# Crossbar transposes of 2048 columns made as two of 1024, and one batch's quantised activations transposed as pairs of bytes

## The chip, the cores and the metric

The kernel runs on one core of a Trainium2 chip. The metric is the device time of one execution in microseconds (us), the median over the runs. A core has five engines, each with an instruction stream of its own: TensorE (PE in the profile, with PEld for its weight loads), VectorE (DVE), ScalarE (ACT), GpSimd (POOL) and SyncE (SP). In this kernel SP issues every DMA, the transposes among them.

## The reference

There are two batches of 1024 tokens by 2048 features. A layer norm is followed by a product with a context matrix, both sides quantised to 0..255; then comes a second layer norm, and a linear layer with a routed LoRA (8 experts, rank 16, the best two). Both steps are added to x:

```python
def fake_quant(x, scale, zp):
    q = jnp.clip(jnp.round(x / scale + zp), 0.0, 255.0)
    return (q - zp) * scale

x = x + fake_quant(layernorm(x)) @ fake_quant(ctx)          # ctx: 2 x 2048 x 2048
y = layernorm(x)
w = top-2 weights of softmax(y @ W_router.T)                # 8 experts
h = einsum('td,erd->ter', y, lora_A)
x = x + y @ W_base.T + b_base + 2 * einsum('ter,eor,te->to', h, lora_B, w)
```

## The kernel before

Tokens go in 8 tiles of 128 (the `i` of the code), pairs of them in 4 (`p`); features and columns go in 16 chunks of 128 (`k`), outputs in blocks of 512 (`c`) or halves of 1024 (`cp`). Everything is done for batch 0 and then for batch 1, and the two overlap at the seam.

**First product.** `ln1` (L628 on) computes the statistics of one x tile (L408 on DVE, a Newton step at L644 that POOL does for all but the first four tiles of batch 0), quantises each half to bytes `q8` with `affine` (L387 if ACT does it, L392 to L398 on DVE), makes fp16 `qn` from them, and turns the tile over, so that features lie on partitions: `at_i`. For the first four tiles of batch 0 TensorE does that (`turn`, L690); for all others one `transpose` of 2048 columns (L377) goes through the crossbar of the DMA engines. In the profile the tiles are named without their numbers: `q`, `qn`, `at`. The context is loaded in pieces of 512 KB (`bs`), quantised to `u` and brought to fp16 as `b` (`load_b`). Batch 0 multiplies plainly (L723, 512 matmuls). Batch 1 uses one level of Strassen-Winograd: `half_sums` makes `as12` and `as4` from pairs of `at` (L797, profile name `as`), `half_diffs` makes `bt` from `b` (L814), and `gemm1w` multiplies (L843, banks `gX` and `gY`, 448 matmuls). The result is added to x as it leaves the bank (L752); squares for the next layer norm are summed on ACT (L771).

**Second product.** `y_prep` (from L888) normalises a pair of tiles and makes seven combinations `a11`, `a12`, `a22`, `s1` to `s4`. Each is split in `emit` into a high and a low fp16 part that stand side by side in a tile `nat` of 2048 columns, and one `transpose` makes a tile `y` from both. In the profile `nat_a` and `y_a` hold the `a` tiles and `nat_s` and `y_s` the `s` tiles. `hmm` multiplies the `a11`, `a12`, `s1`, `a22` tiles by the router and LoRA-A weights (L953 and L957, bank `ph`); `router` picks the experts and builds the weighted hidden tile `hh`, which another transpose turns into `hT`. `g2` is the linear layer, again by Strassen, with three fp16 products for each one (L1281, banks X and Y, 2688 matmuls), the LoRA part at L1297 and the sum into x at L1309. Its weights are prepared by `w_step` for each chunk and group: a load (`wc`, `wt`, `wb`, `wn`), on DVE some differences, a high part (L387 or L394) and a low part (L1091). L532 and L536 belong to a maximum over the LoRA weights that is taken once (`sm_bmax`, `bmax_row`).

**Order.** Nothing in the code says in which order the engines work. Each operation is added to a `Plan` as a task with an engine (or two, DVE and ACT, with a cost for each), the buffers that it reads and writes, sometimes in parts, and for matmuls a due time. `Plan.rank` gives every other task a due time backwards from its readers. `Plan.order` then runs a small model of the core: each engine takes the most urgent task that is ready and whose buffers fit into the slots (48 of 4 KB under tag `u`), and the task stays busy for its cost. The tasks are emitted in the order of their modelled starts, and that is the order of each engine's instructions. For DMAs the model keeps one shared stretch of transfers (`dma_free`, 0.82 us for each 1024 transposed columns) and up to 8 lanes. A transposing SP task is modelled as holding SP for 1.35 us and 0.22 more for each 1024 columns, and until 0.2 us before the latest landing of any DMA issued so far:

```python
if t.turn:
    end = max(end, land - 0.2)
dma_free = max(end + 0.2, dma_free) + t.dma
```

So a change of a cost or of a buffer's parts can move any instruction of SP, ACT and DVE.

Of the kernel before, what the change touches and what calls it, by code (L numbers as in the profile page):

```python
# [15 lines left out]
U8 = mybir.dt.uint8  # L16
AF = mybir.ActivationFunctionType
# [4 lines left out]
P = 128  # L22
# [21 lines left out]
MM = 0.216  # L44
LANES = 8
# [40 lines left out]
TURN_COST = 0.82  # L86
# [22 lines left out]
class Plan:  # L109
# [56 lines left out]
    def order(self):  # L166
# [7 lines left out]
        land = 0.0  # L174
# [44 lines left out]
        while todo:  # L219
# [8 lines left out]
            for eng in busy:  # L228
                while busy[eng] <= now:
                    pick = None  # L230
                    q = ready[eng]
                    for n, item in enumerate(q):
# [9 lines left out]
                        if t.dma is not None:  # L242
# [3 lines left out]
                            if len([x for x in lanes if x > now]) >= LANES:  # L246
                                break
# [19 lines left out]
                    if t.dma is not None:  # L267
                        if t.turn:
                            end = max(end, land - 0.2)
# [4 lines left out]
                        land = max(land, t.done)  # L274
                        lanes = [x for x in lanes if x > now] + [t.done]
# [27 lines left out]
def xattn_ffn_kernel(ctx, tc, x, cx, scal, wT, bias, arT, bT, out):  # L303
# [72 lines left out]
    def transpose(dst, src, r, w, cols, **kw):  # L376
        add("SP", 1.35 + 0.22 * cols / 1024, lambda: nc.sync.dma_start_transpose(dst(), src()),  # L377
            r=r, w=w, dma=TURN_COST * cols / 1024, turn=True, **kw)

    def affine(dst, src, n, r, w, scale=None, bias=None, only=None, **kw):  # L380
# [19 lines left out]
        durs = {"ACT": n * 0.00083 + 0.19 + 0.09 * ptrs, "DVE": n * 0.00053 + 0.145 + 0.06 * ptrs}  # L400
        if only:
# [226 lines left out]
    def ln1(S, b, i):  # L628
# [30 lines left out]
        qn = buf("u", [P, D], F16, f"qn_{n}", 2)  # L659
        for h in range(2):  # L660
            q8 = buf("q8", [P, HD], U8, f"q8_{n}_{h}")
            affine(q8.ap, xt[h].ap, HD, [xt[h], s], [q8],
                   scale=lambda: s.ap()[:, 10:11], bias=lambda: s.ap()[:, 12:13],
                   only=None if b == 0 and i < QBOTH else "ACT")
            affine(lambda h=h: qn.ap()[:, h * HD : (h + 1) * HD], q8.ap, HD, [q8], [(qn, [h])],
                   bias=nz1)
            if pe_turn:
                turn(aT, qn, h, n)
        if not pe_turn:
            transpose(aT.ap, qn.ap, [qn], [aT], D)  # L670
# [29 lines left out]
    def load_b(S, b, c):  # L700
        for j in range(4):
            bp = buf("u", [P, 4, C], F16, f"b_{b}_{c}_{j}", 2)
            S["b", c, j] = bp
            for h in range(2):
# [5 lines left out]
                         "(k p) n -> p k n", p=P), HD * 4, [s])  # L710
# [177 lines left out]
    def y_prep(S, b, p):  # L888
# [10 lines left out]
        def emit(o, t):  # L899
            n = buf("u", [P, 2, HD], F16, f"nat_{o}_{b}_{p}")  # L900
            y = buf("u", [P, 2, HK, P], F16, f"y_{o}_{b}_{p}")
            S["y", p, o] = y
            affine(lambda: n.ap()[:, 0], t.ap, HD, [t], [n])
            add("DVE", 1.22,
                lambda: nc.vector.tensor_tensor(
                    n.ap()[:, 1], t.ap(), n.ap()[:, 0], ALU.subtract), r=[t], w=[n])
            transpose(
# [559 lines left out]
```

## Time and profile before

| what | value |
|---|---|
| median of 3 runs | 921.09 us (920.28, 921.09, 923.07) |
| the profiled execution, its own time | 919.79 us |
| its span in the trace | 918.0 us |
| mean granted TensorE clock | 0.994 of full speed |
| DMA, mean over the span | 265 GB/s |
| `y_s<-nat_s` transposes | 32, median 4.7 us from issue to landing |
| `y_a<-nat_a` transposes | 24, median 5.1 us |
| `at<-qn` transposes | 12, median 5.8 us |
| `hT<-hh` transposes | 2, median 6.0 us |
| context loads `bs` | 64 of 512 KB, median 10.6 us |

The page of the profile shows one execution. Its first part gives the busy time of each engine as a share of the span. The timeline view lists the instructions of an engine in order: start, time, engine, line, operation, output and inputs with their shapes, how many of the same kind are put together on the row, and in brackets the idle time before it with what ended it. "SPq" rows are DMA issues on SP's queue; their time is how long SP itself was held, not how long the transfer took. The waits view adds up the idle time of an engine by what it waited for. Matmuls are pipelined, so that a row's duration can be longer than the distance to the next one.

### The profile page before, as it was taken

The page shows a single profiled execution, that of the slowest core. Times are in us where ns is not written, and L with a number is a line of the kernel's source. Part 1 is how long each engine was busy: PE and PEld are TensorE (multiplying, and loading weights), DVE is VectorE, ACT ScalarE, POOL GpSimd, SP SyncE. Part 2 cuts the span into 40 slices and gives each one's busy share as a digit, 9 for nine tenths or more (in the row PEclk, how much of TensorE's full clock was granted, in tenths as well). Part 3 has the DMA queues.
Part 4 walks back from the last instruction along what each step waited for, and adds up shares of the span by engine and source line. Part 5 has one row for each costly group of instructions (what it writes and reads, how often), then busy time and mean ns, then how long its engine had stood idle before and what let it go on. Part 6 is the DMA issues. An engine that isn't in the chain of part 4 may idle for free. (4 is left out here: it accounts for less than half of the span.)

```text
span 918.0 us, 12390 instructions
## 1 busy us (share of the span) xinstructions
PE 897.9 (98%) x4514; PEld 430.2 (47%) x4514; DVE 712.2 (78%) x1267; ACT 401.5 (44%) x458; POOL 66.1 (7%) x256
## 2 busy tenths in 40 slices
PE   7999999999999999999998999999999999999998
PEld 5444445474444444444443444647444444444443
DVE  7999998989598975999978998999835353799131
ACT  5999676516064321423892575863200121234000
POOL 0024220000000000002621003000000000000000
PEclk8999999999999999999999999999999999999999
DMA  9999999998999999999999946999995169793021
GB/s 321 387 385 284 314 289 251 180 225 267 235 332 321 391 393 374 380 381 342 315 319 243 366 179 158 243 230 211 307 260 186 58 203 389 245 353 127 12 91 47
DMA packets 230733, 243.11 MB, mean 265 GB/s; under 512 B 152848, under 2 KB 165136, under 8 KB 230672
## 3 DMA queue, kind: packets, MB, share of 16 engines
q1 hardware_dynamic: 230672, 242.33, 87.0%
q8 instruction: 35, 0.57, 0.2%
q14 instruction: 26, 0.21, 0.1%
HBM read 163.65 MB, written 41.94 MB: 224 GB/s over the span
## 5 line engine op out<-in xcount | busy, mean ns | idle before, releaser
L1281 PEld LDWEIGHTS <-y_s 128*128 128x128 f16 x1536 | 150.1, 98 | 183.4 <-issue 2.8
L1281 PE MATMUL X<-w,y_s 128*128 128x512 f16 x768 | 207.2, 379 | 2.0 <-DVE w L1091 2.0
L1281 PE MATMUL Y<-w,y_s 128*128 128x512 f16 x768 | 207.0, 379 | 0.0
L1281 PE MATMUL X<-w,y_a 128*128 128x512 f16 x768 | 189.2, 379 | 0.0
L1281 PEld LDWEIGHTS <-y_a 128*128 128x128 f16 x1152 | 112.0, 98 | 133.0 <-DMA y_a<-nat_a 1.3
L723 PE MATMUL g<-b,at 128*128 128x512 f16 x512 | 114.6, 384 | 4.1 <-ACT b L387 2.0
L387 ACT ACTIVATE w<-wb,gW 128x1024 f16<-128x1024 f32 (+1 forms) x48 | 51.5, 1076 | 121.5 <-DVE wb L1152 56.6
L1281 PE MATMUL Y<-w,y_a 128*128 128x512 f16 x384 | 103.2, 379 | 0.3 <-DMA y_a<-nat_a 0.3
L723 PEld LDWEIGHTS <-at 128*128 128x128 f16 x512 | 50.1, 99 | 64.4 <-issue 4.4
L1309 DVE SCALAR_TENSOR_TENSOR xr<-X,uW,xr 128x512 f32<-128x512 f32 x64 | 46.5, 746 | 30.4 <-PE X L1297 24.0
L1309 DVE SCALAR_TENSOR_TENSOR xr<-Y,uW,xr 128x512 f32<-128x512 f32 x42 | 31.1, 745 | 46.7 <-PE Y L1297 30.9
L1091 DVE SCALAR_TENSOR_TENSOR w<-wb,gW,w 128x1024 f16<-128x1024 f32 (+1 forms) x48 | 56.9, 1193 | 8.1 <-ACT w L387 7.8
L435 POOL TENSOR_TENSOR sm<-sm 128x1 f32<-128x1 f32 (+1 forms) x48 | 14.2, 296 | 487.2 <-DVE sm L421 484.7
L771 ACT ACTIVATE sq<-x,sm 128x1024 uint8<-128x1024 f32 x32 | 36.4, 1139 | 25.7 <-DVE x L752 16.7
L387 ACT ACTIVATE b<-u,nz 128x1024 f16<-128x1024 uint8 x41 | 45.7, 1138 | 1.8 <-DVE bt L814 0.8
L387 ACT ACTIVATE u<-bs,sc,rec 128x1024 uint8<-128x1024 f32 x31 | 38.0, 1233 | 15.4 <-DMA bs<-in_cx_dram 14.5
L408 DVE BATCH_NORM_STATS2 sm<-x 128x6 f32<-128x512 f32 x64 | 40.9, 683 | 4.8 <-DMA x<-in_x_dram 4.8
L387 ACT ACTIVATE w<-wt,gW 128x1024 f16<-128x1024 f32 x14 | 16.1, 1148 | 64.7 <-DVE wt L1138 41.6
L387 ACT ACTIVATE q<-x,sm 128x1024 uint8<-128x1024 f32 x30 | 35.7, 1229 | 13.3 <-POOL sm L644 8.6
L387 ACT ACTIVATE nat_s<-yt_a 128x1024 f16<-128x1024 f32 x30 | 31.1, 1050 | 19.4 <-DVE yt_a L912 13.2
L843 PEld LDWEIGHTS <-at 128*128 128x128 f16 x256 | 24.9, 98 | 31.0 <-issue 1.2
L912 DVE TENSOR_TENSOR yt_a<-yt_a,yt_a 128x1024 f32<-128x1024 f32 x32 | 38.6, 1220 | 0.0
(188 smaller groups left out, 1158.7 us busy)
## 6 DMA issues: line engine op xcount, KB each, us to landing
bs<-in_cx_dram SPq DMA_DIRECT2D x64, 512.0 KB, 10.6
wt<-in_wT_dram SPq DMA_DIRECT2D x64, 512.0 KB, 7.6
wn<-in_wT_dram SPq DMA_DIRECT2D x32, 512.0 KB, 9.0
x<-in_x_dram SPq DMA_DIRECT2D x30, 512.0 KB, 7.7
spill<-x SPq DMA_DIRECT2D x28, 512.0 KB, 4.4
xr<-spill SPq DMA_DIRECT2D x28, 512.0 KB, 8.1
wb<-in_wT_dram SPq DMA_DIRECT2D x24, 512.0 KB, 8.0
out_dram<-xr SPq DMA_DIRECT2D x24, 512.0 KB, 6.1
```

The costliest lines, as they stand in the source:

```text
L387: nc.scalar.activation(o, i, AF.Copy if c is None else AF.Identity, scale=1.0 if a is None else a, bias=0.0 if c is None else c,)
L408: nc.vector.bn_stats(st[:, 2 * h + c], b.ap()[:, c * C : (c + 1) * C])
L435: e.tensor_tensor(t, r, r, ALU.mult)
L723: nc.tensor.matmul(ps.ap(), aT.ap()[:, k, :], S["b", c, k // 4].ap()[:, k % 4, :], start=k == 0, stop=k == KT - 1,)
L771: nc.scalar.activation(sq.ap(), xb.ap(), AF.Square, bias=a[:, 22 + j : 23 + j], accum_out=a[:, 24 + 2 * j + h : 25 + 2 * j + h],)
L843: nc.tensor.matmul(ps.ap(), a()[:, 4 * h + k, :], w.ap()[:, k, :], start=fresh and h + k == 0, stop=h == 1 and k == 3, skip_group_check=True,)
L912: add("DVE", 1.22, lambda: nc.vector.tensor_tensor(dst.ap(), a.ap(), c.ap(), op), r=[a, c], w=[dst])
L1091: lambda: nc.vector.scalar_tensor_tensor(w.ap()[:, 1, lo:up], src(), g, w.ap()[:, 0, lo:up], ALU.mult, ALU.subtract),
L1281: nc.tensor.matmul(ps.ap(), y.ap()[:, a, k, :], w.ap()[:, q, j * C : (j + 1) * C], start=k == 0 and fresh and i == 0, stop=k == HK - 1 and ...
L1309: nc.vector.scalar_tensor_tensor(xs, ps.ap(), uW[:, cp : cp + 1], xs, ALU.mult, ALU.add)
```

## The change

A transpose never has more than 1024 columns. The late x tiles of batch 0, all `y` tiles and `hT` are turned over in two halves, each with its own part of the buffers, so that a reader of one half waits for that half alone. In `emit` the high half is issued before the low part is computed; the two halves of `y` are its high and its low part. In `router` the two halves are tiles 0 to 3 and 4 to 7, and the LoRA matmuls at L1297 name the half that they read.

For batch 1, x isn't brought to fp16 ahead of the transpose. ACT quantises both halves into one byte tile `q`; its 2048 bytes in a row are read as 1024 16-bit values and turned over once, so that a partition then holds two neighbouring features, byte by byte. Two `affine`s unpack every second byte into the fp16 tile `at`. The features therefore stand in another order within each group of 256, and batch 1's context rows are loaded in that order too, two neighbouring rows to a partition.

The planner's model gets new constants. A transpose holds SP for 1.5 us, and 1024 columns take 1.0 us of transfer in place of 0.82. SP is no longer held until the latest landing, only until there is room in a ring of 5, of which a transpose takes 2 and any other DMA 1. An unpack is costed at 0.75 us on DVE.

```diff
--- before.py
+++ after.py
@@ -14,6 +14,7 @@
 I32 = mybir.dt.int32
 U32 = mybir.dt.uint32
 U8 = mybir.dt.uint8
+U16 = mybir.dt.uint16
 AF = mybir.ActivationFunctionType
 ALU = mybir.AluOpType
 AX = mybir.AxisListType
@@ -42,6 +43,7 @@
          "sm": 4, "sm2": NP, "wacc": 1, "ps": 8}
 HORIZON = 120.0
 MM = 0.216
+SPREAD = .75
 LANES = 8
 DEPTH = 2.5
 NEAR = 45.0
@@ -83,7 +85,10 @@
 LAND = 2.1
 STORE_LAND = 1.15
 TURN_LAND = 0.65
-TURN_COST = 0.82
+TURN_COST = 1.0
+TURN_ISSUE = 1.5
+RING = 5
+TURN_RING = 2
 NEXT = {"DVE": 0.08, "ACT": 0.1}
 
 
@@ -171,7 +176,6 @@
         events = [0.0, 0.9]
         lanes = []
         dma_free = 1.2
-        land = 0.0
         lag = 0.0
         for t in self.tasks:
             t.left = len(t.preds)
@@ -243,7 +247,7 @@
                             if dma_free > now + DEPTH:
                                 wake(dma_free - DEPTH)
                                 break
-                            if len([x for x in lanes if x > now]) >= LANES:
+                            if len([x for x in lanes if x[0] > now]) >= LANES:
                                 break
                         if (eng == "DVE" and len(t.durs) > 1 and busy["ACT"] <= now
                                 and t.prio > -100):
@@ -266,13 +270,18 @@
                     end = now + t.dur
                     if t.dma is not None:
                         if t.turn:
-                            end = max(end, land - 0.2)
+                            room = RING - TURN_RING
+                            for at, n in sorted(lanes, reverse=True):
+                                room -= n
+                                if room < 0:
+                                    end = max(end, at)
+                                    break
                         dma_free = max(end + 0.2, dma_free) + t.dma
                         t.done = dma_free + (
                             TURN_LAND if t.turn else STORE_LAND if t.store else LAND
                         )
-                        land = max(land, t.done)
-                        lanes = [x for x in lanes if x > now] + [t.done]
+                        lanes = [x for x in lanes if x[0] > now]
+                        lanes.append((t.done, TURN_RING if t.turn else 1))
                     else:
                         t.done = end + 0.1
                         end -= NEXT.get(eng, 0.0)
@@ -374,10 +383,10 @@
             r=r, w=w, dma=nbytes * P / RATE, **kw)
 
     def transpose(dst, src, r, w, cols, **kw):
-        add("SP", 1.35 + 0.22 * cols / 1024, lambda: nc.sync.dma_start_transpose(dst(), src()),
+        add("SP", TURN_ISSUE, lambda: nc.sync.dma_start_transpose(dst(), src()),
             r=r, w=w, dma=TURN_COST * cols / 1024, turn=True, **kw)
 
-    def affine(dst, src, n, r, w, scale=None, bias=None, only=None, **kw):
+    def affine(dst, src, n, r, w, scale=None, bias=None, only=None, dve=None, **kw):
         ptrs = sum(v is not None and not isinstance(v, float) for v in (scale, bias))
 
         def fn(eng):
@@ -398,6 +407,8 @@
                 nc.vector.tensor_scalar(o, i, a, c, ALU.mult, ALU.add)
 
         durs = {"ACT": n * 0.00083 + 0.19 + 0.09 * ptrs, "DVE": n * 0.00053 + 0.145 + 0.06 * ptrs}
+        if dve:
+            durs["DVE"] = dve
         if only:
             return add(only, durs[only], lambda: fn(only), r=r, w=w, **kw)
         return add(durs, 0, fn, r=r, w=w, **kw)
@@ -656,18 +667,39 @@
             add("DVE", 0.6, lambda: rstd_seed(s, 1), w=[s])
             add("DVE" if fast else "POOL", 1.6 if fast else 4.0, newton, w=[s])
         aT = buf("u", [P, KT, P], F16, f"at_{n}", 2)
-        qn = buf("u", [P, D], F16, f"qn_{n}", 2)
-        for h in range(2):
-            q8 = buf("q8", [P, HD], U8, f"q8_{n}_{h}")
-            affine(q8.ap, xt[h].ap, HD, [xt[h], s], [q8],
-                   scale=lambda: s.ap()[:, 10:11], bias=lambda: s.ap()[:, 12:13],
-                   only=None if b == 0 and i < QBOTH else "ACT")
-            affine(lambda h=h: qn.ap()[:, h * HD : (h + 1) * HD], q8.ap, HD, [q8], [(qn, [h])],
-                   bias=nz1)
-            if pe_turn:
-                turn(aT, qn, h, n)
-        if not pe_turn:
-            transpose(aT.ap, qn.ap, [qn], [aT], D)
+        if b:
+            q = buf("u", [P, 2, D], U8, f"q_{n}", 4)
+            for h in range(2):
+                affine(lambda h=h: q.ap()[:, 0, h * HD : (h + 1) * HD], xt[h].ap, HD, [xt[h], s],
+                       [(q, [h])], scale=lambda: s.ap()[:, 10:11], bias=lambda: s.ap()[:, 12:13],
+                       only="ACT")
+            transpose(
+                lambda: q.ap()[:, 1].bitcast(U16).rearrange("p (k t) -> p k t", t=P),
+                lambda: q.ap()[:, 0].bitcast(U16), [(q, [0, 1])], [(q, [2, 3])], HD)
+            for h in range(2):
+                affine(
+                    lambda h=h: aT.ap()[:, h * HK : (h + 1) * HK, :].rearrange(
+                        "p (k s) t -> p k s t", s=2),
+                    lambda h=h: q.ap()[:, 1, h * HD : (h + 1) * HD].rearrange(
+                        "p (k t s) -> p k s t", t=P, s=2),
+                    HD, [(q, [2 + h])], [(aT, [h])], bias=nz1, dve=SPREAD)
+        else:
+            qn = buf("u", [P, D], F16, f"qn_{n}", 2)
+            for h in range(2):
+                q8 = buf("q8", [P, HD], U8, f"q8_{n}_{h}")
+                affine(q8.ap, xt[h].ap, HD, [xt[h], s], [q8],
+                       scale=lambda: s.ap()[:, 10:11], bias=lambda: s.ap()[:, 12:13],
+                       only=None if b == 0 and i < QBOTH else "ACT")
+                affine(lambda h=h: qn.ap()[:, h * HD : (h + 1) * HD], q8.ap, HD, [q8], [(qn, [h])],
+                       bias=nz1)
+                if pe_turn:
+                    turn(aT, qn, h, n)
+            if not pe_turn:
+                for h in range(2):
+                    transpose(
+                        lambda h=h: aT.ap()[:, h * HK : (h + 1) * HK, :],
+                        lambda h=h: qn.ap()[:, h * HD : (h + 1) * HD], [(qn, [h])], [(aT, [h])],
+                        HD)
         S["at", i] = aT
         if first:
             warm = bank("warm")
@@ -707,7 +739,7 @@
                 s = buf("u", [P, 2, C], F32, f"bs_{b}_{c}_{j}_{h}")
                 load(s, s.ap,
                      cx[b, k0 * P : (k0 + 2) * P, c * C : (c + 1) * C].rearrange(
-                         "(k p) n -> p k n", p=P), HD * 4, [s])
+                         "(p k) n -> p k n" if b else "(k p) n -> p k n", p=P), HD * 4, [s])
                 u = buf("u8", [P, 2, C], U8, f"u_{b}_{c}_{j}_{h}")
                 affine(u.ap, s.ap, HD, [s], [u], scale=r2, bias=z2)
                 affine(lambda bp=bp, h=h: bp.ap()[:, h * 2 : h * 2 + 2, :], u.ap, HD, [u],
@@ -897,16 +929,20 @@
             return t
 
         def emit(o, t):
-            n = buf("u", [P, 2, HD], F16, f"nat_{o}_{b}_{p}")
-            y = buf("u", [P, 2, HK, P], F16, f"y_{o}_{b}_{p}")
+            n = buf("u", [P, 2, HD], F16, f"nat_{o}_{b}_{p}", 2)
+            y = buf("u", [P, 2, HK, P], F16, f"y_{o}_{b}_{p}", 2)
             S["y", p, o] = y
-            affine(lambda: n.ap()[:, 0], t.ap, HD, [t], [n])
+
+            def turn_half(a):
+                transpose(lambda: y.ap()[:, a], lambda: n.ap()[:, a], [(n, [a])], [(y, [a])], HD)
+
+            affine(lambda: n.ap()[:, 0], t.ap, HD, [t], [(n, [0])])
+            turn_half(0)
             add("DVE", 1.22,
                 lambda: nc.vector.tensor_tensor(
-                    n.ap()[:, 1], t.ap(), n.ap()[:, 0], ALU.subtract), r=[t], w=[n])
-            transpose(
-                lambda: y.ap().rearrange("p h k t -> p (h k) t"),
-                lambda: n.ap().rearrange("p h c -> p (h c)"), [n], [y], D)
+                    n.ap()[:, 1], t.ap(), n.ap()[:, 0], ALU.subtract),
+                r=[t, (n, [0])], w=[(n, [1])])
+            turn_half(1)
 
         def comb(dst, a, c, op):
             add("DVE", 1.22, lambda: nc.vector.tensor_tensor(dst.ap(), a.ap(), c.ap(), op),
@@ -977,7 +1013,7 @@
         hf = S["hf"]
         rt = buf("u", [P, NT * 76], F32, f"rt_{b}")
         hh = buf("u", [P, NT, 2, ER], F16, f"hh_{b}")
-        hT = buf("u", [P, NT, 2, P], F16, f"hT_{b}")
+        hT = buf("u", [P, NT, 2, P], F16, f"hT_{b}", 2)
         S["hT"] = hT
 
         def cut(o, *shape):
@@ -1045,9 +1081,12 @@
             lambda: nc.vector.tensor_tensor(
                 hh.ap()[:, :, 1], hf.ap()[:, :, :ER], hh.ap()[:, :, 0], ALU.subtract),
             r=[hf], w=[hh])
-        transpose(
-            lambda: hT.ap().rearrange("p t h c -> p (t h) c"),
-            lambda: hh.ap().rearrange("p t h c -> p (t h c)"), [hh], [hT], D)
+        for q in range(2):
+            ts = slice(q * NT // 2, (q + 1) * NT // 2)
+            transpose(
+                lambda ts=ts: hT.ap()[:, ts].rearrange("p t h c -> p (t h) c"),
+                lambda ts=ts: hh.ap()[:, ts].rearrange("p t h c -> p (t h c)"),
+                [hh], [(hT, [q])], HD)
 
     made = {}
     STORED = {
@@ -1300,7 +1339,7 @@
                         skip_group_check=True,
                     )
 
-            add("PE", 3 * MM, lmm, r=[hT, lb], w=[ps], prio=t + 6 * MM)
+            add("PE", 3 * MM, lmm, r=[(hT, [(2 * p + tt) // 4]), lb], w=[ps], prio=t + 6 * MM)
         for bk, tt, c in EVAC[f][grp]:
             ps, xb = S[bk, p], S["c", cp, 2 * p + tt]
```

## The prediction, made before the change was run

> **What bounds the kernel now.** I read the page's busy shares first, then the matmul rows of the PE timeline, then PE's waits, then SP's queue beside each wait. The page's first part:
>
> ```profile
> PE 897.9 (98%) x4514; PEld 430.2 (47%) x4514; DVE 712.2 (78%) x1267; ACT 401.5 (44%) x458; POOL 66.1 (7%) x256
> ```
>
> TensorE is busy for 98% of 918.0 us, and the change leaves its instructions as they are: the order comparison has 9018 PE rows on both sides. So nothing can be won but PE's stalls. I measured these in the PE timeline as the distance from one matmul's start to the next, less 0.216 us per 512 columns (the pitch of unbroken runs; a row's duration is pipelined and says less). They add up to 25.7 us, 12.9 of them in the first 30 us. All engines keep their instructions and order for about the first 75 us (the first differences are ACT's 53rd, SP's 56th, DVE's 144th and PE's 910th row), so those 12.9 stay. The 4.4 us after the last matmul (913.6 to 918.0) stay too. About **12 us** after 75 us can be had, in few places. The waits of PE name them (in us: total, times, longest; those that belong to the first 75 us are left out):
>
> ```profile
> PE X L1281 <- DVE w L1091: 2.0, 3, 0.9
> PE gY L843 <- DVE as L797: 1.7, 2, 1.4
> ...
> PE gX L843 <- DVE as L797: 1.6, 1, 1.6
> PE ph L953 <- DMA y_a<-nat_a: 1.5, 1, 1.5
> PE bmax_row L536 <- DVE sm_bmax L532: 1.1, 1, 1.1
> ...
> PE gX L843 <- DVE x L752: 0.5, 1, 0.5
> PE Y L1297 <- DMA hT<-hh: 0.3, 1, 0.3
> PE Y L1281 <- DMA y_a<-nat_a: 0.3, 1, 0.3
> ```
>
> Start to start, with their places: A 98.8-102.4, bmax, 1.24. B 146.9-148.6, first lora matmuls on a transposed y, 1.63. C 257-276, w of batch 0's first FFN half, 2.49 in three stalls. D 287, hT, 0.49. E 487-500, batch 1's gemm1, 3.98. G 570, x, 0.64. H 605-608, y of batch 1, 0.60. Five smaller ones hold 0.8 together. Sum 11.9.
>
> B, D and H wait for a transpose itself. C and E hang on one indirectly, through SP, which issues every load, store and transpose in turn. C's queue (start, us, then the instruction):
>
> ```profile
> 227.45 4.79 SPq L377 DMA_TRANSPOSE y_s<-nat_s  x1
> 232.34 0.53 SPq L373 DMA_DIRECT2D wc<-in_wT_dram  x1
> 232.96 13.21 SPq L377 DMA_TRANSPOSE y_s<-nat_s  x5
> 246.26 0.67 SPq L373 DMA_DIRECT2D bb<-in_bias_dram  x1
> ```
>
> A load leaves SP in about 0.5 us, a transpose holds it for 2 to 5. Eight transposes hold it from 221.92 to 246.26, and the w loads behind them come late for L1091 at 257. At E it is worse:
>
> ```profile
> 465.53 0.91 SPq L373 DMA_DIRECT2D x<-in_x_dram  x1
> 466.55 7.84 SPq L377 DMA_TRANSPOSE at<-qn  x1
> 474.43 2.11 SPq L373 DMA_DIRECT2D bs<-in_cx_dram  x4
> 477.99 0.36 SPq L1224 DMA_DIRECT2D out_dram<-xr  x1
> 478.44 9.32 SPq L377 DMA_TRANSPOSE at<-qn  x2
> ```
>
> With six DMAs outstanding a 2048 transpose held SP for 7.84 us, until one was left. Elsewhere too it went on only then: from seven outstanding after 11.0, from five 7.36, from two mostly 2.8 to 4.8, from one 1.8 to 2.9. So the queue drains at each one, and what is issued next starts with a gap.
>
> **Part 1: 2048 made as 1024s.** 70 transposes become 132: 8 for batch 0's late x, 112 for y, 4 for hT, and 8 for batch 1's x (part 2). SP has 62 instructions more.
> - *Transfer.* Back to back, 2048s land 2.4 to 2.6 us apart (238.48, 241.05, 243.51, 246.01, 248.31). A half moves half the packets, so I take 1.2, and the same sum. Bounds: 0.9, if fewer broken runs give the best packet rate I saw (567 in 0.5 us against 425); 1.9, if a half holds SP as long as a whole back-to-back 2048 does at its quickest (1.83 and 1.85 us). I take 1.2, as nothing in these landings shows a fixed part.
> - *SP.* 70 hold it for 225.7 us, 3.22 on average, mostly by draining. 132 at 1.2 would be 158, at 1.9 251. Whether a half needs a drained queue is not shown; it asks for half the descriptors. Nothing lost: 1.2 behind a full queue. As before: a drain each.
> - *A rule against it.* The Trainium skill, "DMA: Bandwidth & Descriptors", section "Anatomy of one DMA", gives a fixed cost of about 2.0 us to each DMA on GpSimd's path, so 62 more would be 124 us if they ran singly. The rows above bear on it: a y_s takes a median 4.7 us from issue to landing, yet the next lands 2.4 behind it. That fixed part overlaps in a full queue. It would show only where one half runs alone.
> - *y.* The high half goes out before the low part (L905, 1.22 us on DVE) exists; the low half's chain gets shorter by one half's transfer.
> - *Order.* The planner now holds SP by ring room and not by the last landing, and it moves all of SP, ACT and DVE after 75 us (POOL's order is the same). I therefore compared the emitted lists: how many us of matmul (at 0.216) lie between a producer's place and its first reader on PE. A small lead is a stall.
>
> **Part 2: batch 1's x as byte pairs.** Gone: 8 transposes of 2048 and 16 affines u8 to fp16 ahead of them (ACT 1134 ns, DVE 750). New: 8 transposes of 1024 columns, and 16 unpacks behind them, 13 on ACT and 3 on DVE. On DVE the source has a stride of two bytes, which no row shows: lower end 750 ns (same types, unit stride), upper end 1220 (L912, which has two f32 sources). I take 750, the nearest row; the upper end is 3 x 0.47 = 1.4 us of DVE. The price: the unpack stands behind the transpose, 0.75 to 1.13 us more between landing and as (L797), against 1.2 less transfer: even. 8 x 1.2 = 10 us of DMA are saved where the DMA share is full (443 to 503). The ctx rows are read in another order in 2 KB pieces as before: nothing. "VectorE: DVE Perf Modes", section "What auto-detection actually checks" asks a unit step only of the 16-bit packing, which would leave the unpack at the lower end; no row here shows it.
>
> **The sum, stall by stall** (leads before and after in us of matmul):
> - A: sm_bmax 0.00 to 3.46; 1.24 becomes 0.1. **-1.1** (0 to -1.2)
> - B: the second half of y_a12 has 11.2 instead of 6.4. Next late is the first w: its L1091 ended at 148.80, and PE would be there at 150.04 - 1.63 = 148.4. 0.6 stays. **-1.0** (0 to -1.6)
> - C: the w's 0.00, 1.94, 1.30 become 1.30, 2.59, 1.94. A lead of 1.3 is about one L1091 (1.2). Half stays. **-1.2** (+2.5 to -2.5)
> - D: the second half of hT isn't read first. **-0.3** (0 to -0.5)
> - E: bt2 .86-1.73 to 1.73-2.59, as12 0.00-.86 to 1.7-3.5, the first b of group 1,2 from 0.00 to .86. **-3.0** (0 to -4.0). Its head was on ACT:
>
> ```profile
> 486.67 1.24 ACT L387 ACTIVATE q<-x,sm 128x1024 uint8<-128x1024 f32 x1 [3.55 <-POOL sm L644]
> 487.81 1.22 ACT L387 ACTIVATE u<-bs,sc,rec 128x1024 uint8<-128x1024 f32 x1
> ```
>
> ACT stood 3.55 us for the last x's statistics (its load had left at 465.53, and landed at 474.71 behind the drain), and a ctx tile was queued behind; DVE's b then idled 3.29 for u. In the new order ACT has the ctx tiles and two unpacked tiles ahead of that q.
> - G, H: G's x stays. Batch 1's y_a leads go from 4.2-7.1 to 3.3-7.8. Half's issue to landing, 4.7 - 1.2 = 3.5, is about the smallest of them. H goes, G may grow. **-0.6** (+1.5 to -1.2)
>
> Together -7.2. New orders bring new stalls, which leads don't show if DVE or ACT is late: A to H average 11.1/7 = 1.6 us; I take one, **+1.6** (0 to 4). Net -5.6. The profiled execution took 919.79 (span 918.0 and 1.8 around it): **914.2**; the median shown, 921.09, is 1.3 above that: **915.5**.
>
> **Rivals.**
> 1. *Halves cost more than half* (slower). In C all 16 halves go out in one piece, ahead of the w loads. At 1.9 us that is 16 x 0.7 = 11.2 us more; 1.3 us of lead is there, so 9.9 us would fall on PE: 925.4. At 1.63 a half (16 x 0.43 - 1.3 = 5.6) all of the gain is spent, from 1.81 (16 x 0.61 - 1.3 = 8.4) it is slower by over 0.3%. For it: the quickest unblocked 2048 still took SP 1.34. Against it: the even landings.
> 2. *The stalls move.* DVE is busy for 49.97 of the 60 us at 443-503 and for 72.89 of the 78 us at 119-197. If it is the limit there, B and E stay and only A, C, D and H give: -3.2 + 1.6 = -1.6, 919.5.
> 3. *Nearly all of it goes*: -7.2 with no new stall and C and B at their ends: -9.1, 912.0; the cap is 909.2.
> 4. *It doesn't do what it says*: a half needs the drained queue too. SP then holds 132 times, what part 1 gives is lost, part 2's 10 us of DMA remain: 920 to 924.
>
> **Numbers.** 0.3%, 2.8 us, is about what a measurement of this kernel can tell from no change; so faster is below 918.3, slower above 923.9. Forecast (913 to 918.3) 0.52, rival 3 0.14, rival 2 0.16, rival 4 0.06, rival 1 0.12. Faster .52 + .14 = 0.66; same .16 + .04 = 0.20; slower .12 + .02 = 0.14. The range 911 to 922.5 leaves out rival 1 and the ends.
>
> **What would show it.** SP rows of halves below 1.5 us and no 7 us holds: step 1. Landings of y_s halves 1.2 apart: the transfer; 1.8 or more: rival 1, with w L1091 waits growing at 230-280. Unpack rows on DVE near 750 or 1220. No as or bt wait at 487-500: E; a wait for DVE in their place: rival 2. The prediction is wrong if a stall over 3 us stands at a new place, or if matmul time itself changes.

## The result and the profile after

The changed kernel takes **927.15 us** (median of 8 runs, 924.44 to 930.64) against 921.94 of 8 runs of the kernel before on the same chip: a ratio of **1.0056, 95% interval 1.0035 to 1.0077**. It is slower, by 5.2 us. 915.5 was forecast, and the time lies outside the range of 911 to 922.5. The profiled execution took 927.01 (span 925.2, mean granted clock 0.991). Over all runs the kernel before has a median of 922 to 923; the profile that the prediction was made from (919.79) shows one of its quicker executions.

TensorE's work is what it was; the page's first part of the changed kernel:

```profile
PE 901.1 (97%) x4514; PEld 432.4 (47%) x4514; DVE 708.7 (77%) x1264; ACT 404.3 (44%) x461; POOL 66.1 (7%) x256
```

So the loss, like the gain hoped for, must lie in PE's stalls. Measured as in the prediction (distance of starts less 0.216 us per 512 columns), by 40 us of each kernel's own time:

| stretch, us | before | after | difference |
|---|---|---|---|
| 0-80 | 13.3 | 12.8 | -0.6 |
| 80-120 | 1.4 | 0.1 | -1.3 |
| 120-160 | 1.8 | 7.5 | **+5.6** |
| 240-280 | 2.5 | 1.0 | -1.5 |
| 280-320 | 0.9 | 5.3 | **+4.4** |
| 480-520 | 4.1 | 0.3 | **-3.8** |
| 520-560 | 0.4 | 1.1 | +0.7 |
| 560-600 | 0.6 | 4.9 | **+4.3** |
| 600-640 | 0.6 | 0.0 | -0.6 |
| the rest | 0.0 | 0.2 | +0.2 |
| all | 25.7 | 33.1 | +7.4 |

The gains came in full: 7.8 us. But in four stretches PE stands 15.1 us longer. The waits view of PE after the change (us in total, times, longest) names them:

```profile
PE X L1320 <- DVE w L1130: 3.4, 4, 1.4
PE ph L993 <- DMA y_a<-nat_a: 3.1, 1, 3.1
PE X L1320 <- ACT w L396: 2.4, 1, 2.4
...
PE wsum L604 <- DVE wacc L600: 1.7, 1, 1.7
PE X L1320 <- DVE x L1348: 1.5, 1, 1.5
```

Of the lines shown of before, `as`, `hT` and `bmax_row` are gone (`L843 <- DVE as` is L875 now, and no longer listed). The three new places, in order of time:

**L1, 146-157.** The y wait B is gone, and PE stands 2.56 and 1.60 us for the first FFN weights instead. DVE has no gap there; a Newton step of the next layer norm now runs ahead of the weight scale (L456 at 146.44, before L445 at 144.38), and the low part of the first w comes at 151.0 instead of 148.80. DVE's timeline, two rows of before and then one of after:

```profile
144.38 0.16 DVE L445 TENSOR_SCALAR wacc<-wsum 128x1 int32<-128x1 int32 x1
147.52 1.28 DVE L1091 SCALAR_TENSOR_TENSOR w<-wn,gW,w 128x1024 f16<-128x1024 f32 x1
```

```profile
146.44 0.15 DVE L456 TENSOR_SCALAR wacc<-wsum 128x1 int32<-128x1 int32 x1
```

After the stall the clock drops. Windows view, one row of before and then four of after: window, length, busy us (and instructions) of PE, PEld, DVE, ACT, POOL, then the granted clock, the DMA share and GB/s:

```profile
151.00:157.00 6.00, 6.00 (x30) 2.70 (x29) 6.00 (x6) 5.97 (x7) 0.00 (x0) 1.00 1.05 321
```

```profile
146.00:151.00 5.00, 1.29 (x12) 0.82 (x10) 4.83 (x15) 5.00 (x6) 0.00 (x0) 0.91 1.09 256
151.00:157.00 6.00, 5.87 (x15) 2.07 (x15) 6.00 (x7) 6.00 (x9) 0.00 (x0) 0.51 1.10 273
...
585.00:590.00 5.00, 1.94 (x16) 1.10 (x15) 4.98 (x9) 3.34 (x6) 0.00 (x0) 1.00 1.08 254
590.00:594.00 4.00, 4.00 (x26) 2.93 (x25) 1.15 (x9) 2.07 (x5) 0.00 (x0) 0.57 1.01 192
```

The second row of after has 15 matmuls in 6 us; the same window of before has 30 at clock 1.00. Twelve of the 15 took 427 ns each, which costs 2.5 us in all. In these two profiles no drop follows the stalls of 1.9 us and less. But length alone doesn't decide it: in profiles of other runs below, one stall of 3.08 us left the clock at 1.00 (`before_wclate`, up to 149), and one of 2.12 us brought it to 0.67 over 310 to 315 (`after_wclate`). "TensorE: Matmul & The Clock Gate", Part 1, of the Trainium skill states that about one window of 3.4 us of idling brings half rate. The rows agree on the half rate (427 ns where 216 is usual), but not on the length: every stall named here was shorter than 3.4 us. The prediction's sum didn't price the drop.

**L2, 298-312.** The PE timeline after (in brackets the idle time ahead of a row and what ended it), then SP's queue:

```profile
301.94 3.61 PE L1320 MATMUL X<-w,y_a 128*128 128x512 f16 x16 [1.49 <-DVE x L1348]
...
310.62 0.38 PE L604 MATMUL wsum<-wacc,ones 128*128 128x1 f32 x2 [1.73 <-DVE wacc L600]
```

```profile
295.40 0.33 SPq L382 DMA_DIRECT2D wb<-in_wT_dram  x1
304.28 0.38 SPq L382 DMA_DIRECT2D wn<-in_wT_dram  x1
304.75 0.42 SPq L382 DMA_DIRECT2D wt<-in_wT_dram  x1
```

SP issued nothing from 295.73 to 304.28, 8.55 us: the last `wn` load waits until ACT (L591, 303.10 to 304.25) has read the `wn` ahead of it, which landed at 303.08. ACT's row and the window behind it, both after:

```profile
303.10 1.06 ACT L591 ACTIVATE wn<-wn 128x1024 f32<-128x1024 f32 x1 [5.00 <-DMA wn<-in_wT_dram]
304.00:308.00 4.00, 3.83 (x19) 1.66 (x17) 3.93 (x6) 1.58 (x4) 0.00 (x0) 1.00 0.56 161
```

The DMA share falls from 0.99 in 300-304 to 0.56 in 304-308, and the `wt` behind the `wn` lands at 310.43. Before the change the same load landed at 306.24, because the last `wn` went out at 295.42, while the one ahead of it was still on its way:

```profile
295.42 0.38 SPq L373 DMA_DIRECT2D wn<-in_wT_dram  x1
298.08 0.33 SPq L373 DMA_DIRECT2D wt<-in_wT_dram  x1
```

**L3, 586-594.** SP's queue before, then after:

```profile
572.68 0.57 SPq L373 DMA_DIRECT2D wc<-in_wT_dram  x1
573.66 3.63 SPq L377 DMA_TRANSPOSE y_a<-nat_a  x1
577.38 0.53 SPq L373 DMA_DIRECT2D spill<-x  x1
578.61 7.45 SPq L377 DMA_TRANSPOSE y_a<-nat_a  x3
586.11 5.68 SPq L373 DMA_DIRECT2D wc<-in_wT_dram  x6
```

```profile
568.68 0.54 SPq L382 DMA_DIRECT2D wc<-in_wT_dram  x1
571.98 0.33 SPq L382 DMA_DIRECT2D spill<-x  x1
572.40 2.55 SPq L382 DMA_DIRECT2D wc<-in_wT_dram  x3
576.58 5.94 SPq L386 DMA_TRANSPOSE y_a<-nat_a  x2
582.61 0.53 SPq L382 DMA_DIRECT2D spill<-x  x1
583.23 0.38 SPq L382 DMA_DIRECT2D wc<-in_wT_dram  x1
583.71 9.74 SPq L386 DMA_TRANSPOSE y_a<-nat_a  x6
```

The router needs y_a11 of pair 1. Before, that is the transpose at 573.66, landed at 579.40. After, three `wc` loads (512 KB each) stand ahead of its first half, a store and another `wc` ahead of its second (583.71), which lands at 589.17. PE stood for it, and from 590.4 on ran at half its clock for some 3 us (0.57 over 590 to 594):

```profile
585.88 0.28 PE L989 MATMUL ph<-ar,y_a 128*128 128x272 f16 x1
589.22 0.23 PE L993 MATMUL ph<-ar,y_a 128*128 128x136 f16 x1 [3.06 <-DMA y_a<-nat_a]
```

The halves themselves, in the stretch that answers to C's queue:

```profile
226.78 6.10 SPq L386 DMA_TRANSPOSE y_s<-nat_s  x4
232.97 0.53 SPq L382 DMA_DIRECT2D wc<-in_wT_dram  x1
233.60 14.64 SPq L386 DMA_TRANSPOSE y_s<-nat_s  x10
248.29 0.58 SPq L382 DMA_DIRECT2D bb<-in_bias_dram  x1
```

Ten halves in 14.64 us, against five wholes in 13.21. Unblocked halves hold SP for 1.23 to 1.36 us, and the last eight land 1.36 apart (240.59 to 250.10), as far apart as SP issues them. A pair is 2.72, a whole was 2.46: dearer, but only by 0.26. From the first issue to the landing of `bb` the stretch takes 29.3 us against 28.9 before. At the seam ACT now has other work while it waits for a transpose, and E's stall of 3.98 is 0.25:

```profile
485.27 1.15 ACT L396 ACTIVATE at<-q,nz 128x1024 f16<-128x1024 uint8 x1 [0.97 <-DMA q<-q]
486.32 1.13 ACT L396 ACTIVATE b<-u,nz 128x1024 f16<-128x1024 uint8 x1
487.36 2.17 ACT L396 ACTIVATE at<-q,nz 128x1024 f16<-128x1024 uint8 x2
489.44 1.23 ACT L396 ACTIVATE q<-x,sm 128x1024 uint8<-128x1024 f32 x1
```

### The profile page after: what moved, and what is told of

It reads as the page before. It is cut to its first block, busy times and chain, and to the rows that moved or that the text cites. A ratio compares the mean times of both kernels' runs of the same rounds, so it can differ in the third digit from the quotient of the medians.

```text
span 925.2 us, 12515 instructions
## 1 busy us (share of the span) xinstructions
PE 901.1 (97%) x4514; PEld 432.4 (47%) x4514; DVE 708.7 (77%) x1264; ACT 404.3 (44%) x461; POOL 66.1 (7%) x256
## 4 chain that ended last, share of the span: by engine, by line
PE 71%; DVE 11%; DMA 10%; ACT 4%; issue 2%; POOL 1%; SPq 1%; DVEq 0%; ACTq 0%
PE X L1320 30%; PE Y L1320 24%; PE g L755 6%; DMA wn<-in_wT_dram 4%; PE ph L989 2%; PE gX L875 2%; DMA q<-q 2%; PE gY L875 2%; DVE x L784 2%; PE X L1336 1%; PE ph L993 1%; PE Y L1336 1%; DMA lbs<-in_bT_dram 1%; ACT at L396 1%; DMA wb<-in_wT_dram 1%
## 5 line engine op out<-in xcount | busy, mean ns | idle before, releaser
L1320 PE MATMUL X<-w,y_a 128*128 128x512 f16 x768 | 191.8, 382 | 6.5 <-DVE w L1130 2.6
L1320 PEld LDWEIGHTS <-y_a 128*128 128x128 f16 x1152 | 113.0, 99 | 142.0 <-issue 12.1
L446 POOL TENSOR_TENSOR sm<-sm 128x1 f32<-128x1 f32 (+1 forms) x48 | 12.2, 253 | 490.0 <-DVE sm L432 484.0
L396 ACT ACTIVATE w<-wt,gW 128x1024 f16<-128x1024 f32 x16 | 18.0, 1145 | 64.5 <-DVE wt L1177 40.0
L396 ACT ACTIVATE nat_s<-yt_a 128x1024 f16<-128x1024 f32 x28 | 28.8, 1051 | 27.9 <-DVE yt_a L948 23.9
L396 ACT ACTIVATE yt_a<-x,sm 128x1024 f32<-128x1024 f32 x26 | 31.1, 1232 | 20.4 <-POOL sm L916 12.1
L875 PEld LDWEIGHTS <-at 128*128 128x128 f16 x256 | 24.9, 98 | 30.9 <-issue 1.4
```

The source lines that it names most:

```text
L396: nc.scalar.activation(o, i, AF.Copy if c is None else AF.Identity, scale=1.0 if a is None else a, bias=0.0 if c is None else c,)
L446: e.tensor_tensor(t, r, r, ALU.mult)
L875: nc.tensor.matmul(ps.ap(), a()[:, 4 * h + k, :], w.ap()[:, k, :], start=fresh and h + k == 0, stop=h == 1 and k == 3, skip_group_check=True,)
L1320: nc.tensor.matmul(ps.ap(), y.ap()[:, a, k, :], w.ap()[:, q, j * C : (j + 1) * C], start=k == 0 and fresh and i == 0, stop=k == HK - 1 and ...
```

## The experiments

Theory **O**: the planner's new order costs the time, by what stands ahead of what on SP. Rivals: **C**, PE's stalls and the clock drop after them (L1, L3) cost it by themselves; the halves cost it (rival 1 of the prediction). Ratios are to the kernel before, run beside each one, with 95% intervals; each median is of 6 to 12 executions.

**1. Filling the stalls.** `fill_stalls` gives PE 36 spare matmuls of 256 columns ahead of the first FFN matmul, and 31 of 240 columns in the router, so that it doesn't idle at L1 and L3. They compute nothing that is used.

```diff
+                if (b, f, grp, k, p, j) == (0, 0, 0, 0, 0, 0):
+                    for _ in range(36):
+                        nc.tensor.matmul(
+                            ps.ap()[:, : 2 * P], ones.bitcast(F16)[:, :P], ones.bitcast(F16),
...
+            if (b, i, half) == (1, 2, 0):
+                for _ in range(31):
```

> After, with the same order on every engine, but 36 spare matmuls of 256 columns (3.9 us) ahead of the first FFN matmul of batch 0, where PE stood 4.2 us at 147-151, and 31 of 240 columns (3.1 us) ahead of the router matmul of batch 1 that waited 3.2 us at 586. They compute nothing that is used. Theory C (the stall itself brings a second loss: after it the granted clock fell to 0.51 over 151-157 and 0.57 over 590-594): the clock stays near 1.0 there, the matmuls behind go at 216 ns, and the time falls by 2.5 + 1.6 = about 4 us, to 923. Rival: the slow matmuls behind the stalls have another reason (operands or queues that fill up after a stall): the two windows stay as slow, and the time stays at 927 or rises by what the spare matmuls overrun.

Measured: **927.92**, 1.0058 [1.0037, 1.0078], no change. The clock stayed up, as its windows view shows:

```profile
151.00:157.00 6.00, 6.00 (x29) 2.74 (x28) 6.00 (x7) 6.00 (x8) 0.00 (x0) 1.00 1.19 288
590.00:594.00 4.00, 2.94 (x33) 2.56 (x34) 1.00 (x7) 2.05 (x4) 0.00 (x0) 1.00 0.98 207
```

But what PE won at 157, 3.0 us, it lost at the next w, in the PE timeline of the same run:

```profile
258.51 0.38 PE L1332 MATMUL X<-w,y_s 128*128 128x512 f16 x1 [0.30 <-ACT w L396]
261.25 0.59 PE L1332 MATMUL X<-w,y_s 128*128 128x512 f16 x2 [2.36 <-DVE w L1136]
```

After 240 us of matmul work (the spare ones not counted) both kernels stand at the same time (261.86 and 261.90). DVE, which makes that w, had itself stood 4.91 us for the landing of `bb` (at 253.5; in the changed kernel at 252.8). At L3 nothing was won either: the same matmuls, 556 to 563 us of work, took 11.6 us against 11.8. In this order what comes next on the DMA queue sets PE's time, and C falls.

**2. The two halves of the change apart.** `split_only` is the changed kernel with batch 1's x in fp16 halves; `bytes_only` is the kernel before with the byte pairs alone (old planner rule, wholes); `before_newplan` has the new planner rule and costs alone.

```diff
 split_only, against after
-        if b:
+        if b > 9:
...
 before_newplan, against before
...
-                            end = max(end, land - 0.2)
+                            room = RING - TURN_RING
+                            for at, n in sorted(lanes, reverse=True):
...
```

> After without the byte pairs: batch 1's x is brought to fp16 ahead of the transpose as before, and turned over in two halves of 1024. All of batch 0 has the same order as after. Theory O (the halves are cheap, the loss lies in the new order at 146-157, 300-317 and 586-594): the first two places lose the same 12 to 13 us of PE time as after, the gemm1 seam at 487-500 is good as well (leads 1.7 to 9.5), so 925 to 929. Rival B (the byte pairs cost: unpacks, or ctx in another row order): the time comes back to 921 or below. Rival H (each half costs): y_s halves land 1.6 us or more apart when back to back.

> Before with the byte pairs alone: y, hT and batch 0's x keep their transposes of 2048, and the planner keeps its old rule and costs. All of batch 0 has the order of before. Theory O: batch 0 stalls as before (A, B, C, D); at the seam as and bt have leads of 0.0 to 1.7, as before, so 2 to 4 us of stalls remain at 487-500: 919 to 922. Rival B (the byte pairs cost): 924 or more, with the extra stalls at 440-510 only.

> Before with the planner's new rule and costs, and its 2048-column transposes: nothing else. Until the first FFN the order is nearly after's. Theory O: the place at 146-157 is as bad as in after, or worse by the 2048s that hold SP for up to 11 us against a rule that expects less; so 925 to 935. Rival H (the halves cost, the rule does not): near 921 or below, and no stall over 2 us at 146-157.

Measured: `split_only` **934.08**, 1.0120 [1.0094, 1.0146], worse than expected: it has little of the seam's gain (PE stands 2.52 us for `as` there), so that gain is the byte pairs', not the split's:

```profile
506.07 1.04 PE L875 MATMUL gX<-bt,as 128*128 128x512 f16 x4 [2.52 <-DVE as L829]
```

`bytes_only` **923.96**, 1.0004 [0.9987, 1.0020], above the 919 to 922 expected: the seam wins 4.1 us (matmuls 465 to 475, by us of matmul work, take 10.2 instead of 14.2), and at 586 two waits, 2.47 for w and 1.18 for y_a, take it back. (Its profiled execution, 928.48, was the slowest of its twelve.) `before_newplan` **939.56**, 1.0183 [1.0159, 1.0208]: the new rule lets wholes queue up, SP is held by one for up to 11 us, and stalls of 5.1 us stand at 213 and 505. An order alone is worth 17 us here.

**3. L3.** `after_wclate` lets batch 1's `wc` loads go out at most 12 us of matmul ahead of their due time instead of 90; `bytes_wclate` and `before_wclate` do the same to `bytes_only` and to the kernel before.

```diff
-                s = kept.pop((cp, k), None) or load_wcol(k, cp, 0, f"wc_{n}", far=WFAR)
+                s = kept.pop((cp, k), None) or load_wcol(k, cp, 0, f"wc_{n}", far=12.0 if b else WFAR)
```

> After, but the first weight loads of batch 1's FFN (wc) may not be issued more than 12 us ahead of their due time, so that two of them and not four or five stand ahead of pair 1's y_a transposes on SP, as in before; batch 0 is unchanged. Theory Q (the order of SP's queue: four 512 KB loads and a spill ahead of the y_a halves made them land at 589.2, where before's landed at 579.4): the wait of 3.2 us at 586 and the slow clock behind it (1.7) go, so about -4.6: 922.5. Rival D (DVE's low parts at 581-586 come too late, whatever SP does): a wait of 2 us or more stays there, 925 to 927.

> The byte pairs alone (2048-column transposes, the old rule) with the same late wc loads. Theory Q: the seam's 4 us stay won (465 to 475 us of matmul time took 10.2 us with the pairs and 14.2 without) and the loss at 586-589 (5.2 us) goes: 918 to 920, some 0.4% under before. Rival R (what the seam gains is taken back at the next late place, wherever that is): a new wait of 3 to 4 us within 500-620, 922 to 925.

> Before with the late wc loads alone. Its own order had only two wc loads ahead of the y_a transposes, so theory Q expects no change, 921 to 923; the 3 us by which the byte pairs with late wc loads beat before would then be the byte pairs' own. Rival L (the late wc loads are what wins): 919 to 920.

Measured: `after_wclate` **924.49**, 1.0022 [1.0010, 1.0034], by the ratios 0.34% or 3.1 us less than after, where 4.6 was hoped for: the 3.2 at 586 is 0.3, and 1.2 us of wait come at 592. The 2 us or more of rival D don't stay there. In its SP queue the half that was late goes out at 579.98 instead of 583.71:

```profile
575.07 3.25 SPq L386 DMA_TRANSPOSE y_a<-nat_a  x2
578.42 0.53 SPq L382 DMA_DIRECT2D spill<-x  x1
579.04 0.40 SPq L382 DMA_DIRECT2D wc<-in_wT_dram  x1
579.98 9.32 SPq L386 DMA_TRANSPOSE y_a<-nat_a  x6
```

`bytes_wclate` **919.43**, 0.9956 [0.9941, 0.9971]: faster than both kernels. `before_wclate` **924.50**, 1.0031 [1.0014, 1.0048]: late `wc` loads by themselves win nothing. The gain of `bytes_wclate` needs both: the byte pairs win it at the seam, and the later loads keep it.

**4. Do the halves cost it?** `s_whole` turns the s tiles over in 2048s (the planner takes 2.4 us of SP for each), all else as after; `split_b0` and `split_b1` are the version with late `wc` and byte pairs, with halves (and the ring rule) in batch 0 or batch 1 only.

```diff
+            whole = o[0] == "s"
...
+            if whole:
+                transpose(
+                    lambda: y.ap().rearrange("p h k t -> p (h k) t"),
+                    lambda: n.ap().rearrange("p h c -> p (h c)"), [n], [y], D)
```

> After, but the s1 to s4 tiles of y are turned over in one transpose of 2048 again, once both parts are there. Theory Q with measured pitches (back to back, halves land 1.37 us apart and wholes 2.46, so 16 halves take 21.9 us and 8 wholes 19.7): batch 0's stretch of eight y_s transposes ends 2 us sooner, the w loads behind it land 2 us sooner, and 1 to 2 us of the loss up to 320 go: 925 to 926. Rival W (a whole costs SP its drain of the queue, and that is worse than 0.27 us a pair): the stretch ends no sooner, and the time is 927 or more.

> The complement: byte pairs, late wc loads, halves of 1024 in batch 0 only, 2048s in batch 1. Theory Q: batch 0 as after's (320 us at 292 us of matmul time, 4 us behind), nothing won later: 923 to 925. Rival S (batch 1's halves are what costs): 919 to 921.

> The byte pairs, the late wc loads, and halves of 1024 in batch 1 only (y and hT there); batch 0 keeps its transposes of 2048 under the old rule, with before's order. Theory Q: batch 0 arrives at its last weight group as before's (some 316 us at 292 us of matmul time, where all kernels with halves in batch 0 came at 320), the seam is good, and batch 1's halves neither win nor lose much: 919 to 921. Rival S (halves in batch 1 cost by themselves): 923 or more, with new waits for y or w within 560-620.

Measured: `s_whole` **925.59**, 1.0026 [1.0008, 1.0044]. The time is as expected, the reason isn't: `bb` behind the s tiles lands at 253.00, in the changed kernel at 252.77, so the wholes won nothing where they are. What its profile does win lies at L2: in its order SP doesn't stand there for long (the last `wn` goes out at 300.57), and matmuls 279 to 292, by us of work, take 13.1 us instead of 16.6. `split_b0` **922.75**, 1.0006 [0.9988, 1.0023], and `split_b1` **921.62**, 0.9991 [0.9975, 1.0008]: neither shows a gain over `bytes_wclate` without halves; but each also has an order of its own, so the 2 to 3 us are not laid to the halves.

**5. L2.** The `wn` tasks are due `WN1` us of matmul ahead of a place in the second half. 50 makes them earlier, 38 later.

```diff
-WN1 = 40.0
+WN1 = 38.0
```

> As after_wclate, and the loads for the second weight norm (wn) are due 10 us sooner. In after SP was held from 295.7 to 304.3 at the last of them, waiting for its slot, and everything behind landed 4.2 to 5.3 us later than before's. Theory Q: no such hold near 295-304, the group 3 weights land 2 to 3 us sooner, 919 to 920. Rival F (the DMA queue is full from 250 to 320 whatever the order, so an earlier wn load only displaces a wc load): the time at 320 stays, 922 to 923.

> As after_wclate, with the wn loads due 2 us later instead of 10 sooner: SP's order up to 250 is the same, the last two wn loads get other buffer slots. Theory Q2 (the 3 to 4 us between 300 and 317 come from SP standing 8.5 us for the slot of its last wn load): SP doesn't stand there, the 12.4 to 17.7 us that 279 to 292 of matmul time took become 13 to 14, and the time falls by 3: 921 to 922. Rival F (the DMA queue is simply full, and the wait only moves): the hold may go, but the time stays at 924 to 925.

> The changed kernel with WN1 = 38 in place of 40, and nothing else; batch 1's wc loads stay where they are. If the SP hold at 296-304 is a place of the loss by itself (L2), the time falls from 927.15 by the 3.8 us that the same edit gave with late wc loads: 923 to 924, and the stall at 586 (3.2) stays. If the 3.8 us came only together with the late wc loads, 926 to 928.

> The kernel before with WN1 = 38. Its matmuls 279 to 292 took 13.3 us, 0.8 of them stalls, so there is little to win. If WN1 = 38 mends the changed kernel's own hold: within 1.5 us of before (920.5 to 923.5), or slower, as any other new order. If it helps whatever the order: 918.5 or less.

> The best version so far (wholes, byte pairs, late wc loads, 919.4) with WN1 = 38. Its matmuls 279 to 292 took 14.1 us. If WN1 = 38 mends only the changed kernel's hold: 918.5 to 921. If it helps whatever the order: 916.5 or less.

Measured: with 50, **924.42**, 1.0019 [1.0006, 1.0032], no gain: SP's stand is gone, but the earlier loads displace `wc` and PE stands 1.99 and 2.22 at 260 and 262. With 38, **920.70**, 0.9986 [0.9971, 1.0001]. `after_wn38`, which has only this edit, **924.12**, 1.0012 [0.9993, 1.0032]: by the ratios 0.44% or 4.1 us less than after. Its SP queue at the place of L2:

```profile
294.24 0.38 SPq L382 DMA_DIRECT2D wn<-in_wT_dram  x1
294.72 0.41 SPq L382 DMA_DIRECT2D wt<-in_wT_dram  x1
299.14 0.33 SPq L382 DMA_DIRECT2D wb<-in_wT_dram  x1
299.59 0.38 SPq L382 DMA_DIRECT2D wn<-in_wT_dram  x1
```

The last `wn` goes out at 299.59, and SP never stands over 4.1 us here. Matmuls 279 to 292 (same measure) took 13.1 us; 16.6 after the change, 13.3 before. Of the two PE rows shown under L2 only the wait for `wacc` goes; two waits for x like the one at 301.94 stay in `after_wn38` (1.36 and 1.93 us, up to 298.55 and 301.13), so SP's stand wasn't their cause. The controls: `before_wn38` **923.77**, 1.0012 [0.9996, 1.0028], and `bytes_wclate_wn38` **918.35**, 0.9957 [0.9940, 0.9975], both as without it. So 38 isn't a better number for any order; it mends what the changed kernel's order broke.

The two places add up nearly: L2 0.44% and L3 0.34% singly, 0.70% together (1.0056 to 0.9986), **6.5 us** of the 7.2 that the sum would be. Each of these three differences is known to some 2.5 us either way, if the intervals of its two ratios are taken as independent. Where each kernel's profiled execution spent its time, by us of matmul work done (0.216 for 512 columns, so that a row means the same matmuls in every kernel; "both" is `after_wclate_wn38`):

| matmuls | place | before | after | `after_wn38` | `after_wclate` | both | `bytes_wclate` |
|---|---|---|---|---|---|---|---|
| 0-128 | A | 143.9 | 142.0 | 142.2 | 142.0 | 141.8 | 143.2 |
| 128-145 | B, L1 | 19.0 | 24.7 | 22.9 | 23.5 | 23.2 | 21.8 |
| 145-292 | C, D, L2 | 150.3 | 153.3 | 150.6 | 154.9 | 152.7 | 151.2 |
| 465-475 | E | 14.2 | 10.2 | 10.2 | 10.2 | 10.1 | 10.1 |
| 556-563 | L3 | 7.1 | 11.8 | 12.0 | 8.4 | 8.3 | 8.2 |

A column is one execution, and executions of one order differ. Seven profiled kernels have the old order in the second row's place: 19.0 in before is the least of them, the others took 20.5 to 24.9, with a median of 21.7. (PE stood 1.6 us for y_a at 146 in before, and 2.5 to 3.1 in four of the others; in `split_b1` and `bytes_only` it stood twice, for 4.4 and 4.7 us together.) Seven with the changed kernel's order there took 21.9 to 24.7, median 23.5. So L1 costs some 2 us and not 5.6, and with ranges that overlap even that isn't shown. The third row is clearer: five kernels with before's order up to 433 us took 148.0 to 151.3, four with the changed kernel's up to 443 us took 153.3 to 155.0. So is E: 10.1 to 11.6 in all profiles with the byte pairs, 12.9 to 17.5 without.

## Why the prediction was wrong, point by point

**Right:** what bounds the kernel, and that only some 12 us of stalls could be had. A gave 1.2 (forecast 1.1), C 1.5 (1.2), D 0.5 (0.3), E 3.7 (3.0), G and H 1.2 (0.6): 8.1 where 6.2 was forecast. B's y wait of 1.6 went too. The halves landed 1.36 apart against 1.2 taken, inside the bounds and far from rival 1's 1.8. The unpacks took 747 ns on DVE (forecast 750) and 1136 on ACT; the upper end of 1220 is out. The 747 ns agree with the Trainium skill, "VectorE: DVE Perf Modes", section "What auto-detection actually checks", as the prediction read it. What would show E right came: no `as` or `bt` wait stands at 487-500.

**Off in size:** SP was to be held for 158 us; it was held for 225.0 by 132 halves, as by 70 wholes before (225.7). A half alone is quick, but behind a full queue it still waits (up to 6.9 us; six holds over 4 us, before twelve). This cost nothing that I could find. What the prediction left open, whether a half needs a drained queue, is answered: all 70 wholes before went on with one other DMA outstanding or none, but 46 of the 132 halves with two or more.

**The step that failed** is the last of the sum: "New orders bring new stalls, which leads don't show if DVE or ACT is late: A to H average 11.1/7 = 1.6 us; I take one, **+1.6** (0 to 4)". The profile showed three, which with the clock's drop make up nearly all of the 15.1 us. Of these 6.5 us at L2 and L3 were shown by taking them away; what L1 costs isn't shown. The sign of being wrong that the prediction named also came: a stall over 3 us at a new place (L3, 3.2). The reasons:
- *The number.* The stalls of the old order were averaged, and that says nothing on those of a new one. `before_newplan` shows what a rule may do: +17 us.
- *What a lead doesn't see.* It was written that leads don't show DVE or ACT being late. L2 and L3 are neither. A lead counts matmul time between a producer's place and its reader; it doesn't count the three 512 KB loads that stand ahead of the producer on SP (L3), nor a load that must wait for a buffer slot, with the whole queue behind it (L2). What stood ahead of the halves at L3 was in the emitted list of SP before the run: "G may grow" named the y_a leads of batch 1, and not that. Whether L2's wait for a slot could have been read there too wasn't tried.
- *B.* "Next late is the first w ... 0.6 stays" took w from the old order (148.80; less its 148.4 that would be 0.4). In the new one DVE does a Newton step first, and w is ready at 151.0. The next late thing moved as well.
- *Stalls don't add up singly.* `fill_stalls` won 3.0 us at 157, and all of it was gone at 261. There an early gain became a longer wait behind the next DMA load; that the plain sum of -7.2 was too much for the same reason is likely, but no run shows it.

Of the rivals, "The stalls move" (0.16) is the nearest, but with the wrong place and size: DVE was not the limit at E, and it gave 919.5. None of them had SP's order as its mechanism, though the prediction says that the planner "moves all of SP, ACT and DVE after 75 us".

**Open:** why the planner puts `wc` loads ahead of y_a11, and the last `wn` behind the slot of the one before it, was not separated into split, costs and ring rule; no run shows what an order fit to the halves would give. With both places mended the change stands at 0.9986 [0.9971, 1.0001], some 4 us short of the forecast; what its profile shows there is L1 and two stalls of 1.8 and 1.9 us at 297 to 302, and these weren't taken away by themselves.

## What to carry to other kernels

Where a planner decides the order, a change of a cost is a new kernel: compare the lists of every queue around each reader that has little slack, and ask of each transfer that a reader will wait for what stands ahead of it on its queue and which of those must wait for a slot. Price the new stalls from the worst such places, not from the average of the old ones. And try the parts alone: here the byte pairs, with batch 1's `wc` loads later, win 0.4% (`bytes_wclate`, 919.43), and the split, which was most of the edit, isn't shown to win anything.

## What the runs showed of the hardware

- A transpose of 1024 columns held SP for 1.23 us at its quickest, one of 2048 for 1.34: the hold hardly fell with the size. Back to back, two halves cost 2.7 us where one whole landed every 2.46.
- Each of the 70 transposes of 2048 columns in the kernel before held SP until at most one other DMA was outstanding; behind seven that took 11.0 us. After the change 46 of 132 halves went on with two or more.
- PE's granted clock was 0.51 over 6 us after two stalls of together 4.2 us, 0.57 over 4 us after one of 3.2, and the same after one of 2.7 (`bytes_wclate`, 149 to 153); one of 2.1 also cost clock (0.67 over 5 us, `after_wclate`). But one of 3.1 cost none (`before_wclate`), nor did two of 1.9 and 1.6 close together in `split_b0`, which in `after_wclate` did (0.57 over 151 to 155).
- One wait varies a good deal between executions: with the kernel before's order at that place PE stood 1.6 to 4.7 us for y_a at 146 in seven profiles, so a stall of 1.6 in a single profile is not its usual price.
